# Block 1 of a two-block transformer: a step of the attention becomes a pair of heads on both sequences, in an order written out by hand

## The chip, the cores and the metric

The kernel runs on one core of a Trainium2 chip. The metric is the device time of one execution in microseconds (us). A profiled execution gives a trace: which instruction ran on which engine from when to when. Engines: PE (TensorE matmuls), PEld (its weight loads), DVE (VectorE), ACT (ScalarE), POOL (GpSimd), SP (SyncE, which issues the DMAs here). PSUM has eight banks of 128 partitions x 512 f32 numbers, into which PE writes.

## The reference

Sixteen sequences of 256 tokens with 128 channels go through two blocks. Block 0 (a feature-map attention and a six-layer local transformer as its feed-forward part) is not touched. Block 1, which the change rewrites, computes, for each sequence:

```
h = layernorm(x) * (1 + ca) + sa
q = (h @ Wq) in 16 heads of 64, * 64**-0.5;  k, v = h @ Wkv   # one k and v for all heads
sim = q @ k.T + relative_bias[head] * 8;  sim[j > i] = -max
x = x + ga * (softmax(sim) @ v, heads joined, @ Wout + bout)
h = layernorm(x) * (1 + cb) + sb
x = x + gb * (gelu(h @ w1 + b1) @ w2 + b2)                    # 128 -> 512 -> 128
```

The six vectors per sequence (`sa`, `ca`, ...) are worked out at the start of the kernel and stand in `mods`. Everything is f32.

## The kernel before

A **unit** is two sequences: x as a 128 x 512 tile, channels on partitions, the tokens of both sequences side by side. There are `NU` = 8 units. Block 0 runs first, in an order fixed by the program (`tc.manual_schedule`); its last stage leaves its result in tiles `z`, and x itself stands in DRAM (`xhome`).

**Between the blocks** (L1174 to L1187) x of all eight units is loaded (L1176, on SP), and the block's gated result is added in four DVE instructions per unit (L1182; `zpart` gives the two halves of the channels). After that block 1's weights are loaded on SP: `cWk` (two DMAs, L1205), `cWv`, `cWq` (L1200), the relative bias of the 8 head pairs in 32 DMAs (L1220, L1221), `cWo`, `dW1`, `dW2`: 38 DMAs. Their buffers come free when block 0's last matmuls are done.

**Block 1** (L1189 to L1435) works on 128 steps: unit, half of the head pairs `g`, sequence `s`, pair `j` in the half. Outside `manual_schedule` the program's order is only a wish: a list scheduler orders each engine's instructions. Its helpers:

- `prepare(u)`: layernorm and modulation (`normed` L227, `modulated` L256: mean by a matmul L230, subtraction on DVE L232, square on ACT L234, variance by matmuls L238, the power -0.5 on POOL L248, widened on POOL L215, transposed on PE L222, multiplied L253, scaled and shifted into `h` L261), then K (L1239, copied by ACT L1241) and V (L1244, L1252).
- `queries(p, h)`: one matmul for a pair of heads and both sequences (L1257), copied and scaled by ACT (L1259). Six buffers.
- `scores(p, s, ...)`: for one pair on one sequence four matmuls into two "sim" banks (L1271; of three), one bank per head; DVE adds the bias and takes the negated maximum in one instruction (L1285), ACT takes the exponential with its sum (L1296), DVE the reciprocal (L1305), POOL multiplies (L1307).
- `flip`: the probabilities are transposed, three 128 x 128 blocks per head into a bank of 384 columns (L1321), copied by DVE for one head (L1324) and by ACT for the other (L1326).
- `attend`: for four pairs together the product with V (L1334), copied by DVE (L1345) and ACT (L1347).
- The output projection is merged matmul by matmul over the next eight steps into a PSUM bank of its own, "y" (L1408).
- `closing(u)`: bias and gated add (L1353, L275 in `gated_add`), layernorm, the MLP (w1 L1362, copied by ACT L1364, gelu in place L1369, w2 L1373, bias L1375), gated add, transposes (L1380), copy (L1384), output DMA.

In a step the loop (L1396 on) first moves each running generator (`prepare` of the next unit, `closing` of the last) by one part, merges one matmul, computes scores, flips the step two back, and attends with the step three back when four pairs are complete. PSUM: four "mm" banks for all passing results, three "sim", one "y".

Of the kernel before, what the change touches and what calls it, by code (L numbers as in the profile page):

```python
# [10 lines left out]
F32 = mybir.dt.float32  # L11
# [33 lines left out]
def adaln_kernel(  # L45
# [9 lines left out]
    psy = ctx.enter_context(tc.tile_pool(name="psy", bufs=1, space=PSUM))  # L55
# [82 lines left out]
    xin = x_tiles(block.enter_context(tc.tile_pool(name="xa", bufs=1)))  # L138
# [87 lines left out]

    def normed(src):  # L227

        pm = bank()
        nc.tensor.matmul(pm, mean128, src, start=True, stop=True)  # L230
        xc = work("xc")
        nc.vector.tensor_tensor(two(xc), src, two(pm), ALU.subtract)  # L232
        sq = work("sqq")
        nc.scalar.activation(sq, xc, AF.Square)  # L234
        yield
        pv = bank()
        for t in range(4):
            nc.tensor.matmul(  # L238
                pv[:, t : t + 1],
                sq[:, t * 128 : (t + 1) * 128],  # L240
                mean128[:, 0:1],
                start=True,
                stop=True,
            )
        ve = small("ve", (128, 4))
        nc.vector.tensor_scalar(ve, pv[:, 0:4], 1e-5, None, ALU.add)
        rs = small("rs", (128, 4))
        nc.gpsimd.tensor_tensor(rs, ve, half[:, 0:4], ALU.pow)  # L248
        ex = widen(rs.unsqueeze(2), 1)
        yield  # L250
        rb = turned(ex)
        xn = work("xn")
        nc.vector.tensor_tensor(xn, xc, rb, ALU.mult)  # L253
        return xn

    def modulated(u, layer, j, dst):  # L256

        xn = yield from normed(two(xin[u]))
        for s in range(2):
            b = 2 * u + s  # L260
            nc.vector.tensor_scalar(  # L261
                dst[:, s * L : (s + 1) * L],
                xn[:, s * L : (s + 1) * L],
                mods[layer][:, j + 1, b : b + 1],
                mods[layer][:, j, b : b + 1],
                ALU.mult,
                ALU.add,
            )
# [904 lines left out]

    xin = x_tiles(ctx.enter_context(tc.tile_pool(name="xb", bufs=1)))  # L1174
    for u in range(NU):
        nc.sync.dma_start(xin[u], xhome[u])  # L1176
        for hf in range(2):
            r, zv = zpart(u, hf)
            for s in range(2):
                b = 2 * u + s  # L1180
                c = slice(s * L, (s + 1) * L)
                nc.vector.scalar_tensor_tensor(  # L1182
                    xin[u][r, c],
                    zv[:, s, :],
                    mods[0][r, 5, b : b + 1],
                    xin[u][r, c],
                    ALU.mult,  # L1187
                    ALU.add,
                )  # L1189


    with ExitStack() as es:
        pss = psum(es, 4, 3)
        wc = es.enter_context(tc.tile_pool(name="wc", bufs=1))
        stage["pool"] = es.enter_context(tc.tile_pool(name="kc", bufs=2))
        at = es.enter_context(tc.tile_pool(name="ct", bufs=2))

# [32 lines left out]

        inputs = {}

        def prepare(u):

            h = ctile("h", (128, 512))
            yield from modulated(u, 1, 0, h)
# [14 lines left out]
            v = ctile("v2", (128, 4, 64))  # L1251
            nc.scalar.copy(v.rearrange("p t d -> p (t d)"), pv[:, 0:256])  # L1252
            inputs[u] = h, kT, v

        def queries(p, h):
            pq = bank()
            nc.tensor.matmul(pq, wq[:, p * 128 : (p + 1) * 128], h, start=True, stop=True)  # L1257
            q = ctile("q2", (128, 512), 6)
            nc.scalar.activation(q, pq, AF.Copy, scale=0.125)  # L1259
            return q  # L1260
# [3 lines left out]
        def scores(p, s, q, kT):  # L1264
# [3 lines left out]
            for t in range(2):  # L1268
                for par in range(2):
                    r = slice(64 * par, 64 * par + 64)  # L1270
                    nc.tensor.matmul(  # L1271
                        sims[par][:, SPANS[t]],
                        q[r, c + 128 * t : c + 128 * t + 128],
                        kT[r, c : c + 128 * (t + 1)],
                        start=True,
                        stop=True,
                    )

# [3 lines left out]
            pr = ctile("pr2", (128, 2, 384), 3)  # L1282
            for par in range(2):
# [11 lines left out]
                for t in range(2):  # L1295
                    nc.scalar.activation(  # L1296
                        pr[:, par, SPANS[t]],
                        lg[:, par, SPANS[t]],
                        AF.Exp,
                        bias=nm[:, t, par : par + 1],  # L1300
                        scale=-1.0,
                        accum_out=ssum[:, t, par : par + 1],
                    )
            rsum = small("rsum2", (128, 2, 2))
# [8 lines left out]
            return pr  # L1313

        def flip(j, pr, prT):

            for par in range(2):
                pt = bank()
                for k in range(3):
                    c = slice(k * 128, (k + 1) * 128)  # L1320
                    nc.tensor.transpose(pt[:, c], pr[:, par, c], ident)  # L1321
                src = pt[:, 0:384].rearrange("p (k q) -> p k q", k=3)
                if par:
                    nc.vector.tensor_copy(prT[:, par, :, j, :], src)  # L1324
                else:
                    nc.scalar.copy(prT[:, par, :, j, :], src)  # L1326

        def attend(s, prT, v, oT):

            for t in range(2):  # L1330
                po = bank()
                for k in range(t + 1):
                    for par in range(2):
# [3 lines left out]
                            prT[:, par, t + k].rearrange("p j q -> p (j q)"),  # L1337
# [11 lines left out]
        def closing(u, oTs):  # L1349


            y = work("yo")
            nc.scalar.activation(y, oTs, AF.Identity, bias=vcol(_C_BOUT))  # L1353
# [3 lines left out]
            yield from modulated(u, 1, 3, h)  # L1357
            yield
            hid = []
            for c in range(4):  # L1360
# [3 lines left out]
                nc.scalar.copy(hc, ph)  # L1364
                hid.append(hc)
                if c % 2:
                    yield
            for c in range(4):
                nc.scalar.activation(hid[c], hid[c], AF.Gelu, bias=vcol(_D_B1 + c))  # L1369
            yield  # L1370
# [3 lines left out]
            y = work("yo")  # L1374
            nc.scalar.activation(y, py, AF.Identity, bias=vcol(_D_B2))  # L1375
            gated_add(u, 1, 5, y)
            yield
# [5 lines left out]
            xo = work("xt", (128, 4, 128))  # L1383
# [7 lines left out]
        steps = [  # L1391
            (u, g, s, j) for u in range(NU) for g in range(2) for s in range(2) for j in range(4)
        ]
        N = len(steps)
        per = N // NU
        for _ in prepare(0):  # L1396
            pass
        qs, prs, prTs, oTs, pys, running, merging = {}, {}, {}, {}, {}, [], []
        n = 0
        while n < N + 3 or running or merging:  # L1400
            for g_ in list(running):
                if next(g_, running) is running:
                    running.remove(g_)
            if merging:
                u, p = merging.pop(0)
                if p == 0:
                    pys[u] = psy.tile([128, 512], F32, tag="y", name="y")
                nc.tensor.matmul(  # L1408
                    pys[u], wout[:, p, :], oTs[u, p // 4][:, p % 4, :], start=(p == 0), stop=(p == 7)
                )  # L1410
                if p == 7:
                    running.append(closing(u, pys.pop(u)))
            if n < N:
                u, g, s, j = steps[n]
                p = 4 * g + j
                h, kT, _ = inputs[u]
                if s == 0:
                    qs[p] = queries(p, h)
                prs[n] = scores(p, s, qs[p], kT)
                if n % per == 4 and u + 1 < NU:  # L1420
                    running.append(prepare(u + 1))
            if 0 <= n - 2 < N:
                u, g, s, j = steps[n - 2]
                if j == 0:
                    prTs[u, g, s] = ctile("prT2", (128, 2, 3, 4, 128))
                    if s == 0:
                        oTs[u, g] = ctile("oT2", (128, 4, 512))
                flip(j, prs.pop(n - 2), prTs[u, g, s])
            if 0 <= n - 3 < N:
                u, g, s, j = steps[n - 3]  # L1430
                if j == 3:
                    attend(s, prTs.pop((u, g, s)), inputs[u][2], oTs[u, g])
                    if s == 1:
                        merging += [(u, 4 * g + a) for a in range(4)]
# [112 lines left out]
```

## Time and profile before

| what | us |
|---|---|
| device time, median of three runs | 4260.83 (4251.34, 4260.83, 4263.39) |
| profiled execution, in all | 4254.63 |
| its span (first to last instruction) | 4252.8 |
| block 1: first scores to the end | 3659.48 to 4252.8 |
| PE, ACT, DVE, POOL busy in the whole span | 3979.4, 2839.5, 2826.8, 2619.5 |

The span is what the trace shows; the rest of the profiled execution lies before and after it. The length of block 1's units is read from the starts of equal groups, such as the four w1 matmuls (L1362) of a unit: 3760.45, 3832.28, 3904.12, 3975.94, 4047.78, 4119.61. A line of the trace's timeline has the start, the time from the first start to the last end of a run of equal instructions, the engine, the line, the operation, result and operands with shapes, the number of instructions, and in brackets how long the engine had been idle and what released it. An f32 matmul is two instructions, so "x8" is four matmuls.

### The profile page before, as it was taken

What the parts mean: (1) busy time and instruction counts of PE and PEld (TensorE: products, weight loads), DVE (VectorE), ACT (ScalarE), POOL (GpSimd) and SP (SyncE); (2) the same over time, 40 slices, a digit from 0 to 9 for tenths busy, and PEclk for the clock granted to TensorE, in tenths of its full rate; (3) what the DMA queues carried; (4) which work ended last, traced back from release to release, by engine and by line L of the source; (5) the groups of instructions that cost most, each with busy time, mean ns of one, the idle gap of its engine ahead of it and who ended that gap; (6) DMA issues with size and microseconds to landing.
All of it is one profiled execution on the core that took longest, in us unless ns stands there. A gap on an engine that the chain in (4) does not pass through costs nothing.

```text
span 4252.8 us, 118394 instructions
## 1 busy us (share of the span) xinstructions
PE 3979.4 (94%) x45491; PEld 2576.8 (61%) x45491; DVE 2826.8 (66%) x6003; ACT 2839.5 (67%) x9800; POOL 2619.5 (62%) x3326
## 2 busy tenths in 40 slices
PE   7867999999999999999999999999999998899998
PEld 4534666666666666666666666666666666454544
DVE  6746667777676777667676767776676765455554
ACT  4535666766767666666766666766667665578785
POOL 5446666676666776676766677666767673343432
PEclk9889999999999999999999999999999999999999
DMA  1334344444444444444444444444444441100000
GB/s 40 40 95 106 100 108 102 113 103 106 109 100 113 106 108 104 106 115 104 104 107 104 114 101 109 106 105 113 105 104 100 108 102 58 46 3 6 4 6 6
DMA packets 193548, 371.06 MB, mean 87 GB/s; under 512 B 42538, under 2 KB 83417, under 8 KB 192985
## 3 DMA queue, kind: packets, MB, share of 16 engines
q1 hardware_dynamic: 192984, 363.50, 34.2%
q8 instruction: 360, 5.90, 0.6%
q14 instruction: 204, 1.66, 0.1%
HBM read 127.92 MB, written 8.91 MB: 32 GB/s over the span
## 4 chain that ended last, share of the span: by engine, by line
PE 45%; DVE 23%; ACT 19%; issue 6%; POOL 5%; DMA 1%; SPq 0%; POOLq 0%; DVEq 0%; ACTq 0%
ACT pr L907 10%; PE mm L948 9%; PE sim L885 7%; DVE sent L745 6%; PE mm L764 4%; ACT sq L743 4%; PE mm L930 4%; POOL pr L922 4%; DVE k L748 3%; DVE q L748 3%; PE mm L740 3%; DVE mx L897 2%; PE mm L847 2%; PE mm L1334 2%; DVE nb L899 2%
## 5 line engine op out<-in xcount | busy, mean ns | idle before, releaser
L907 ACT ACTIVATE pr<-sim,nb,rq 128x64 f32<-128x64 f32 x3072 | 1229.5, 451 | 336.9 <-DVE nb L899 328.9
L922 POOL TENSOR_TENSOR pr<-pr,rsum 128x512 f32<-128x512 f32 x384 | 398.3, 1042 | 809.9 <-DVE rsum L920 769.4
L907 ACT ACTIVATION_READ_ACCUMULATOR pr<-sim,nb,rq 128x1 f32 x3072 | 773.9, 252 | 0.0
L969 PEld LDWEIGHTS y<-zx,wvo 128*128 128x128 f32 x6144 | 715.7, 192 | 91.5 <-issue 88.7
L969 PE MATMUL y<-zx,wvo 128*128 128x128 f32 x6144 | 717.5, 275 | 1.3 <-ACT zx L963 1.2
L740 PE MATMUL mm<-z,wqk 128*128 128x512 f32 x1536 | 706.4, 602 | 8.6 <-DMA wqk<-in_L_ffn_Wqkv_dram 6.7
L745 DVE SCALAR_TENSOR_TENSOR sent<-mm,vec,rope 128x512 f32<-128x512 f32 x768 | 570.6, 743 | 118.4 <-ACT sq L743 110.2
L756 POOL TENSOR_TENSOR k<-k,got 128x512 f32<-128x512 f32 x384 | 496.1, 1292 | 0.0
L756 POOL TENSOR_TENSOR q<-q,got 128x512 f32<-128x512 f32 x384 | 487.9, 1271 | 12.7 <-DMA got<-sent 10.6
L837 POOL TENSOR_TENSOR k<-k,kn 128x512 f32<-128x512 f32 x384 | 481.8, 1274 | 19.6 <-DMA kn<-rkh 19.6
L743 ACT ACTIVATE sq<-mm 128x512 f32<-128x512 f32 x768 | 475.0, 618 | 24.0 <-PE mm L740 23.9
L740 PEld LDWEIGHTS mm<-z,wqk 128*128 128x128 f32 x1536 | 278.1, 191 | 323.1 <-issue 237.4
L961 DVE COPY zx<-mm 128x512 f32<-128x512 f32 x384 | 265.6, 692 | 256.7 <-PE mm L948 256.7
L963 ACT COPY zx<-mm 128x512 f32<-128x512 f32 x384 | 225.2, 586 | 287.8 <-PE mm L948 287.8
L1307 POOL TENSOR_TENSOR pr<-pr,rsum 128x256 f32<-128x256 f32 (+1 forms) x256 | 206.1, 826 | 317.3 <-DVE rsum L1305 309.9
L948 PE MATMUL mm<-prT,xw 64*128 64x256 f32 x3072 | 389.5, 390 | 3.4 <-DVE zx L961 2.0
L897 DVE TENSOR_REDUCE mx<-sim 128x8 f32<-128x512 f32 x384 | 263.2, 685 | 176.1 <-PE sim L885 176.1
L948 PEld LDWEIGHTS mm<-prT,xw 64*128 64x128 f32 x3072 | 293.5, 187 | 119.8 <-issue 90.4
L930 PE MATMUL mm<-ident,pr 128*128 128x128 f32 x1536 | 246.2, 284 | 106.5 <-POOL pr L922 76.6
L930 PEld LDWEIGHTS mm<-ident,pr 128*128 128x128 f32 x1536 | 175.4, 143 | 272.3 <-POOL pr L922 243.4
L885 PEld LDWEIGHTS sim<-k,q 64*32 64x32 f32 x24576 | 264.9, 105 | 86.7 <-issue 58.4
L885 PE MATMUL sim<-k,q 64*32 64x64 f32 x24576 | 298.8, 226 | 19.1 <-issue 9.8
(250 smaller groups left out, 6545.2 us busy)
## 6 DMA issues: line engine op xcount, KB each, us to landing
got<-sent SPq DMA_DIRECT2D x1536, 128.0 KB
kn<-rkh SPq DMA_DIRECT2D x768, 128.0 KB
xw<-xw SPq DMA_DIRECT2D x96, 256.0 KB
wqk<-in_L_ffn_Wqkv_dram SPq DMA_DIRECT2D x48, 128.0 KB
bhome<-brow SPq DMA_DIRECT2D x1, 3072.0 KB
wv<-in_L_ffn_Wqkv_dram SPq DMA_DIRECT2D x12, 256.0 KB
wo<-in_L_ffn_Wo_dram SPq DMA_DIRECT2D x12, 256.0 KB
xt<-in_x_dram SPq DMA_DIRECT2D x8, 256.0 KB
```

Source lines behind the costliest of these rows:

```text
L740: nc.tensor.matmul(pp, wqk[:, j, :], xs, start=True, stop=True)
L743: nc.scalar.activation(sq, pp, AF.Square)
L745: nc.vector.scalar_tensor_tensor(two(sent[:, j, :]), two(pp), scale, tab[1], ALU.mult, ALU.mult)
L756: nc.gpsimd.tensor_tensor(r, r, two(got[:, j, :]), ALU.add)
L837: nc.gpsimd.tensor_tensor(k, k, two(kn), ALU.mult)
L885: nc.tensor.matmul(sims[par][32 * c : 32 * c + 32, c0 : c0 + 64], q[r, s, t0 : t0 + 32], k[r, s, t0 : t0 + 64], start=False, stop=True, sk ...
L897: nc.vector.tensor_reduce(mx, sim.rearrange("p (b k) -> p b k", b=8), AX.X, ALU.max)
L907: nc.scalar.activation(pr[:, x, st, par, :], sims[par][:, b * 64 : (b + 1) * 64], AF.Exp, bias=nbs[par][:, b : b + 1], scale=rn[:, par, b ...
L922: nc.gpsimd.tensor_tensor(prf, prf, rsum.unsqueeze(2).to_broadcast([128, 8, 64]), ALU.mult)
L930: nc.tensor.transpose(pt[:, st * 128 : (st + 1) * 128], pr[:, x, st].rearrange("p h k -> p (h k)"), ident,)
L948: nc.tensor.matmul(pz[par][:, w * 256 : (w + 1) * 256], xw[r, (2 * k + w) % 8, :], prT[r, :, 64 * k + 32 * w : 64 * k + 32 * w + 32], star ...
L969: nc.tensor.matmul(py[:, j * 128 : (j + 1) * 128], vo[:, h, :], zx[:, h % 2, h // 2, :], start=(h == 0), stop=(h == 2 * NP - 1), skip_grou ...
```

## The change

Block 1 goes under `manual_schedule` for PE, DVE, ACT and POOL, so each engine runs in program order (SP's DMAs are still placed by the scheduler). The loop is written anew around it:

- A step is one head pair on **both** sequences: 64 steps, 8 per unit. PSUM is four "mm" and four "sim" banks; the "y" bank is closed after block 0. Per step: 8 score matmuls in a row into the four "sim" banks, the query of the next step, twelve transposes of the step before into three full banks of four. DVE copies two of these banks, ACT the middle one.
- The query is scaled and copied by DVE instead of ACT; two buffers.
- `softmax` and `divided` are separate: the reciprocal and the division of the first sequence stand behind the bias reductions of both, those of the second behind the query and the transposes.
- `attend` runs in the steps 6, 7, 9 and 10 after the unit's first. The output projection is the first two parts of `closing`, four matmuls each, in an "mm" bank. gelu reads PSUM and does the copy, four in a row. Five yields stand between w1 and w2 (one in the last unit), and one more ahead of the output.
- The generators run last in a step, after attend.
- x of a unit is loaded in `prepare(u)` (six buffers, in place of eight tiles loaded together), and the four residual updates stand there (`leave`) as a part of their own. `prepare(0)` stands after the weights in the program.

```diff
-    xin = x_tiles(ctx.enter_context(tc.tile_pool(name="xb", bufs=1)))
-    for u in range(NU):
-        nc.sync.dma_start(xin[u], xhome[u])
-        for hf in range(2):
...
+    accum.close()
...
+        es.enter_context(tc.manual_schedule(engines=ENGINES))
+        pss = psum(es, 4, 4)
...
         def prepare(u):
+            xin[u] = ctile("x", (128, 512), 6)
+            nc.sync.dma_start(xin[u], xhome[u])
+            yield
+            leave(u)
+            yield
             h = ctile("h", (128, 512))
...
-            q = ctile("q2", (128, 512), 6)
-            nc.scalar.activation(q, pq, AF.Copy, scale=0.125)
+            q = ctile("q2", (128, 512), 2)
+            nc.vector.tensor_scalar(q, pq, 0.125, None, ALU.mult)
...
-            pr = ctile("pr2", (128, 2, 384), 3)
+            pr = ctile("pr2", (128, 2, 384), 5)
...
+            for g in range(3):
                 pt = bank()
+                for a in range(4):
+                    nc.tensor.transpose(pt[:, a * 128 : (a + 1) * 128], blocks[4 * g + a], ident)
+                dst = prT[:, 4 * g : 4 * g + 4, j, :]
+                src = pt.rearrange("p (k q) -> p k q", k=4)
+                if g == 1:
+                    nc.scalar.copy(dst, src)
                 else:
+                    nc.vector.tensor_copy(dst, src)
...
+            py = bank()
+            for p in range(NP):
+                nc.tensor.matmul(
+                    py, wout[:, p, :], oTs[p // 4][:, p % 4, :], start=(p == 0), stop=(p == NP - 1)
+                )
+                if p == 3:
+                    yield
...
-                nc.scalar.copy(hc, ph)
+                nc.scalar.activation(hc, ph, AF.Gelu, bias=vcol(_D_B1 + c))
                 hid.append(hc)
-                if c % 2:
+            if u + 1 < NU:
+                for _ in range(5):
                     yield
...
+        while n <= N + 4 or running:
+            u, p = divmod(n, NP)
             if n < N:
                 h, kT, _ = inputs[u]
+                sims = [scores(s, q, kT) for s in range(2)]
+                prs[n] = []
+                for s in range(2):
+                    pr, ssum = softmax(p, sims[s])
+                    prs[n].append((pr, ssum))
+                    if s:
+                        divided(*prs[n][0])
+                if n + 1 < N:
+                    u2, p2 = divmod(n + 1, NP)
+                    q = queries(p2, inputs[u2][0])
+            if 0 <= n - 1 < N:
...
+                flip(j, [v[0] for v in prs.pop(n - 1)], prTs[u1, g])
+            if n < N:
+                divided(*prs[n][1])
+            for lag, g, s in ((6, 0, 0), (7, 0, 1), (9, 1, 0), (10, 1, 1)):
+                v, r = divmod(n - lag, NP)
+                if r == 0 and 0 <= v < NU:
+                    attend(s, prTs[v, g], inputs[v][2], oTs[v, g])
...
+            for parts in list(running):
+                if next(parts, running) is running:
+                    running.remove(parts)
+            v, r = divmod(n - 10, NP)
+            if r == 0 and 0 <= v < NU:
+                running.append(closing(v, [oTs.pop((v, g)) for g in range(2)]))
+            if p == 0 and u + 1 < NU:
+                running.append(prepare(u + 1))
             n += 1
```

More of the change, by code (lines that the diff above doesn't have):

```diff
@@ L54, in adaln_kernel @@
     sm = ctx.enter_context(tc.tile_pool(name="sm", bufs=4))
-    psy = ctx.enter_context(tc.tile_pool(name="psy", bufs=1, space=PSUM))
+    accum = ctx.enter_context(ExitStack())
+    psy = accum.enter_context(tc.tile_pool(name="psy", bufs=1, space=PSUM))
     def bank():
@@ L137, in adaln_kernel @@
     psum(block, 7, 0)
-    xin = x_tiles(block.enter_context(tc.tile_pool(name="xa", bufs=1)))
+    xin = dict(enumerate(x_tiles(block.enter_context(tc.tile_pool(name="xa", bufs=1)))))
     stage["pool"] = block.enter_context(tc.tile_pool(name="ka", bufs=3))
@@ L225, in turned @@
         return rb
[L227 to L268, printed above, removed]
     def gated_add(u, layer, j, y):
@@ L1172, in adaln_kernel @@
         stage["flat"] = None
-    xin = x_tiles(ctx.enter_context(tc.tile_pool(name="xb", bufs=1)))
-    for u in range(NU):
-        nc.sync.dma_start(xin[u], xhome[u])
-        for hf in range(2):
[L1178 to L1189, printed above, removed]
+    accum.close()
     with ExitStack() as es:
-        pss = psum(es, 4, 3)
+        es.enter_context(tc.manual_schedule(engines=ENGINES))
+        pss = psum(es, 4, 4)
         wc = es.enter_context(tc.tile_pool(name="wc", bufs=1))
@@ L1196, in adaln_kernel @@
         at = es.enter_context(tc.tile_pool(name="ct", bufs=2))
+        xin.clear()
         def load1(name, shape, src):
@@ L1229, in ctile, with leave @@
             return at.tile(list(shape), F32, tag=tag, name=tag, bufs=bufs)
+        def leave(u):
+            for hf in range(2):
+                r, zv = zpart(u, hf)
+                for s in range(2):
+                    b = 2 * u + s
+                    c = slice(s * L, (s + 1) * L)
+                    nc.vector.scalar_tensor_tensor(
+                        xin[u][r, c],
+                        zv[:, s, :],
+                        mods[0][r, 5, b : b + 1],
+                        xin[u][r, c],
+                        ALU.mult,
+                        ALU.add,
+                    )
@@ new lines, in modulated @@
+        def modulated(u, j, h):
+            pm = bank()
+            nc.tensor.matmul(pm, mean128, xin[u], start=True, stop=True)
+            xc = ctile("xc", (128, 512), 3)
+            nc.vector.tensor_tensor(xc, xin[u], pm, ALU.subtract)
+            sq = ctile("sqq", (128, 512), 1)
+            nc.scalar.activation(sq, xc, AF.Square)
+            yield
+            pv = bank()
+            for t in range(4):
+                nc.tensor.matmul(
+                    pv[:, t : t + 1],
+                    sq[:, t * 128 : (t + 1) * 128],
+                    mean128[:, 0:1],
+                    start=True,
+                    stop=True,
+                )
+            ve = small("ve", (128, 4))
+            nc.vector.tensor_scalar(ve, pv[:, 0:4], 1e-5, None, ALU.add)
+            rs = small("rs", (128, 4))
+            nc.gpsimd.tensor_tensor(rs, ve, half[:, 0:4], ALU.pow)
+            ex = ctile("ex", (128, 4, 128), 1)
+            nc.gpsimd.tensor_copy(ex, rs.unsqueeze(2).to_broadcast([128, 4, 128]))
+            yield
+            rb = bank()
+            for t in range(4):
+                nc.tensor.transpose(rb[:, t * 128 : (t + 1) * 128], ex[:, t], ident)
+            nc.vector.tensor_tensor(xc, xc, rb, ALU.mult)
+            for s in range(2):
+                b = 2 * u + s
+                c = slice(s * L, (s + 1) * L)
+                nc.vector.tensor_scalar(
+                    h[:, c],
+                    xc[:, c],
+                    mods[1][:, j + 1, b : b + 1],
+                    mods[1][:, j, b : b + 1],
+                    ALU.mult,
+                    ALU.add,
+                )
@@ L1231, in adaln_kernel @@
         inputs = {}
         def prepare(u):
+            xin[u] = ctile("x", (128, 512), 6)
+            nc.sync.dma_start(xin[u], xhome[u])
+            yield
+            leave(u)
+            yield
             h = ctile("h", (128, 512))
-            yield from modulated(u, 1, 0, h)
+            yield from modulated(u, 0, h)
+            inputs[u] = [h]
             yield
@@ L1252, in prepare @@
             nc.scalar.copy(v.rearrange("p t d -> p (t d)"), pv[:, 0:256])
-            inputs[u] = h, kT, v
+            inputs[u] += [kT, v]
         def queries(p, h):
@@ L1257, in queries, with scores @@
             nc.tensor.matmul(pq, wq[:, p * 128 : (p + 1) * 128], h, start=True, stop=True)
-            q = ctile("q2", (128, 512), 6)
-            nc.scalar.activation(q, pq, AF.Copy, scale=0.125)
+            q = ctile("q2", (128, 512), 2)
+            nc.vector.tensor_scalar(q, pq, 0.125, None, ALU.mult)
             return q
         SPANS = (slice(0, 128), slice(128, 384))
-        def scores(p, s, q, kT):
+        def scores(s, q, kT):
             c = s * L
@@ L1277, in scores, with softmax @@
                     )
+            return sims
+        def softmax(p, sims):
             lg = ctile("lg2", (128, 2, 384))
@@ L1303, in scores, with divided @@
                     )
+            return pr, ssum
+        def divided(pr, ssum):
             rsum = small("rsum2", (128, 2, 2))
@@ L1312, in scores, with flip @@
                 )
-            return pr
-        def flip(j, pr, prT):
-            for par in range(2):
-                pt = bank()
[L1319 to L1324, printed above, removed]
+        def flip(j, prs, prT):
+            blocks = [
+                pr[:, par, k * 128 : (k + 1) * 128]
+                for pr in prs
+                for par in range(2)
+                for k in range(3)
+            ]
+            for g in range(3):
+                pt = bank()
+                for a in range(4):
[4 more added lines that the diff above has]
+                    nc.scalar.copy(dst, src)
                 else:
-                    nc.scalar.copy(prT[:, par, :, j, :], src)
+                    nc.vector.tensor_copy(dst, src)
         def attend(s, prT, v, oT):
@@ L1336, in attend @@
                             v[:, 2 * s + k, :],
-                            prT[:, par, t + k].rearrange("p j q -> p (j q)"),
+                            prT[:, 6 * s + 3 * par + t + k].rearrange("p j q -> p (j q)"),
                             start=(k == 0),
@@ L1349, in closing @@
         def closing(u, oTs):
-            y = work("yo")
-            nc.scalar.activation(y, oTs, AF.Identity, bias=vcol(_C_BOUT))
+            py = bank()
+            for p in range(NP):
+                nc.tensor.matmul(
+                    py, wout[:, p, :], oTs[p // 4][:, p % 4, :], start=(p == 0), stop=(p == NP - 1)
+                )
+                if p == 3:
+                    yield
+            y = ctile("yo", (128, 512), 1)
+            nc.scalar.activation(y, py, AF.Identity, bias=vcol(_C_BOUT))
             gated_add(u, 1, 2, y)
@@ L1356, in closing @@
             h = ctile("h3", (128, 512), 1)
-            yield from modulated(u, 1, 3, h)
+            yield from modulated(u, 3, h)
             yield
@@ L1363, in closing @@
                 hc = ctile("hid", (128, 512), 4)
-                nc.scalar.copy(hc, ph)
+                nc.scalar.activation(hc, ph, AF.Gelu, bias=vcol(_D_B1 + c))
                 hid.append(hc)
-                if c % 2:
+            if u + 1 < NU:
+                for _ in range(5):
                     yield
-            for c in range(4):
-                nc.scalar.activation(hid[c], hid[c], AF.Gelu, bias=vcol(_D_B1 + c))
-            yield
+            else:
+                yield
             py = bank()
@@ L1373, in closing @@
                 nc.tensor.matmul(py, w2[:, c, :], hid[c], start=(c == 0), stop=(c == 3))
-            y = work("yo")
+            y = ctile("yo", (128, 512), 1)
             nc.scalar.activation(y, py, AF.Identity, bias=vcol(_D_B2))
             gated_add(u, 1, 5, y)
+            yield
             yield
@@ L1382, in closing @@
                 )
-            xo = work("xt", (128, 4, 128))
+            xo = ctile("xo", (128, 4, 128), 1)
             nc.scalar.copy(xo.rearrange("p t d -> p (t d)"), pt)
@@ L1387, in closing @@
             )
[L1391 to L1395, printed above, removed]
+        N = NU * NP
         for _ in prepare(0):
             pass
-        qs, prs, prTs, oTs, pys, running, merging = {}, {}, {}, {}, {}, [], []
+        q = queries(0, inputs[0][0])
+        prs, prTs, oTs, running = {}, {}, {}, []
         n = 0
[L1400 to L1412, printed above, removed]
+        while n <= N + 4 or running:
+            u, p = divmod(n, NP)
@@ L1413, in adaln_kernel @@
             if n < N:
-                u, g, s, j = steps[n]
-                p = 4 * g + j
                 h, kT, _ = inputs[u]
[L1417 to L1423, printed above, removed]
-                if j == 0:
[L1425 to L1434, printed above, removed]
+                sims = [scores(s, q, kT) for s in range(2)]
+                prs[n] = []
+                for s in range(2):
+                    pr, ssum = softmax(p, sims[s])
+                    prs[n].append((pr, ssum))
+                    if s:
+                        divided(*prs[n][0])
@@ new lines, in adaln_kernel @@
+                if n + 1 < N:
+                    u2, p2 = divmod(n + 1, NP)
+                    q = queries(p2, inputs[u2][0])
+            if 0 <= n - 1 < N:
+                u1, p1 = divmod(n - 1, NP)
+                g, j = divmod(p1, 4)
+                if j == 0:
+                    prTs[u1, g] = ctile("prT2", (128, 12, 4, 128))
+                    oTs[u1, g] = ctile("oT2", (128, 4, 512), 3)
+                flip(j, [v[0] for v in prs.pop(n - 1)], prTs[u1, g])
+            if n < N:
+                divided(*prs[n][1])
@@ new lines, in adaln_kernel @@
+            for lag, g, s in ((6, 0, 0), (7, 0, 1), (9, 1, 0), (10, 1, 1)):
+                v, r = divmod(n - lag, NP)
+                if r == 0 and 0 <= v < NU:
+                    attend(s, prTs[v, g], inputs[v][2], oTs[v, g])
+                    if s:
+                        prTs.pop((v, g))
+            for parts in list(running):
[4 more added lines that the diff above has]
+                running.append(closing(v, [oTs.pop((v, g)) for g in range(2)]))
```

## The prediction

> **What bounds the kernel now.** First the engines' busy times in two whole units of block 1 (columns: window, length, then busy us of PE, weight loads, DVE, ACT, POOL, then clock):
>
> ```profile
> 3832.28:3904.12 71.84, 69.51 (x363) 35.97 (x363) 39.61 (x178) 55.29 (x175) 28.96 (x37) 1.00 0.02 5
> 3904.12:3975.94 71.82, 69.50 (x363) 35.97 (x363) 39.53 (x178) 55.30 (x175) 28.94 (x37) 1.00 0.02 5
> ```
>
> PE is busy for 69.5 of 71.83 us, the same in each unit; ACT and DVE have slack. Block 1 takes 593.3 us, from its first scores at 3659.48 to the end at 4252.8; all before it stays as it was. Next, PE's own order in the timeline (start, duration):
>
> ```profile
> 3839.39 1.02 PE L1408 MATMUL y<-oT,cWo 128*128 128x512 f32 x2
> 3840.34 0.93 PE L1271 MATMUL sim<-k,q 64*128 64x128 f32 x8
> 3841.20 0.87 PE L1321 MATMUL mm<-ident,pr 128*128 128x128 f32 x6
> 3841.91 1.02 PE L1408 MATMUL y<-oT,cWo 128*128 128x512 f32 x2
> 3842.86 0.93 PE L1271 MATMUL sim<-k,q 64*128 64x128 f32 x8
> 3844.47 0.77 PE L1321 MATMUL mm<-ident,pr 128*128 128x128 f32 x5 [0.42 <-POOL pr L1307]
> ```
>
> Work of other stages stands between scores and transposes, so PE almost never waits (the table of PE's waits names 2.2 us in a whole unit, the largest for POOL's probabilities, 1.0): with such gaps as the 0.42 and the leads at a change of operation I count 11 us per unit in which it does no row of work; 61 are work. (f32 runs in two rows, "x8" is four matmuls.) Prices from starts: a 512-column matmul 0.86 (3839.39 to 3840.34 less a lead of 0.095), four score matmuls 0.86 (3840.34 to 3841.20), a transpose 0.11. Last, the entry:
>
> ```profile
> 3572.76 3.68 SPq L1176 DMA_DIRECT2D x<-xh  x8
> ...
> 3642.70 0.81 SPq L1205 DMA_DIRECT2D cWk<-in_L_attn_Wkv_dram  x2
> ...
> 3644.28 1.10 PE L230 MATMUL mm<-x,mean 128*128 128x512 f32 x2 [1.72 <-DVE z L984]
> ...
> 3659.48 2.57 PE L1271 MATMUL sim<-k,q 64*128 64x128 f32 x16
> ...
> 3660.17 1.05 SPq L1200 DMA_DIRECT2D dW<-in_L_ffn_w_dram  x2
> ```
>
> x is fetched 70 us ahead; the 38 weight and bias transfers, 0.47 apart, run beside the first layernorm.
>
> **Entry: +23.** In the new program the first unit's x is queued on SP behind those 38, issued near 3661.3. The last of the 38 landed at 3665.5 at some 210 GB/s; x's 256 KB take 1.2 more: 3666.7. L1182's work, which stood in DVE's queue at 3577.7 ahead of block 0's reciprocal at 3581.55, is gone there: PE waited 3.2 for that, I take 1.7 of it: 3665. Then four residual updates (L1182's four at 3644.17 took 1.77) and 0.25 to the next engine: 3667.1. From L230 to the first scores before took 15.2 (3644.28 to 3659.48); one query less now, but an idle PE's slow rows (below) for longer, 0.4 more on balance: 3682.7, **+23.2**. PE has nothing to hide it. The later units' x is issued two steps, some 14 us, ahead of its use, beside idle queues, and costs nothing; without that cover a load's 2 us plus its 1.2 of transfer would stand in front of p2's updates. The bounds: if x landed before the others, +4 (the updates, less the 1.7, plus PE's wake); if x waited its own 2 us and the idle PE ran its rows at half speed through the entry (they took 0.85 instead of 0.43 at 3644 to 3657 already), +27.
>
> **PE's work per unit: 61.6.** Scores: eight in a row are not in the trace of a full unit. Bounds: two groups as now, 1.91, and the merged row of 3659.48, sixteen in 2.57, so 1.29. I take 1.5, between them and nearer the row: 0.3 saved on each of eight steps, 2.5 with leads. Queries, transposes, attend, merge and MLP keep their matmul count. PE has 61.6 per unit if nothing makes it wait; of the 11 us of gaps it loses the queries' second home and about half the leads.
>
> **What makes it wait.** The order is fixed now: a step is 8 scores, the next query, 12 transposes, then attend or the parts of prepare and closing. The prices of the other engines:
>
> ```profile
> L1324 DVE COPY prT<-mm 128x384 f32<-128x384 f32 x128 | 70.8, 553 | 46.8 <-PE mm L1321 46.7
> L1259 ACT ACTIVATE q<-mm 128x512 f32<-128x512 f32 x64 | 37.8, 591 | 13.7 <-PE mm L1257 13.7
> L1345 DVE COPY oT<-mm 128x512 f32<-128x512 f32 x32 | 21.9, 685 | 32.5 <-PE mm L1334 32.5
> L275 DVE SCALAR_TENSOR_TENSOR x<-yo,mod,x 128x256 f32<-128x256 f32 x32 | 20.2, 670 | 18.9 <-ACT yo L1375 14.3 <-ACT yo L1353 4.6
> L1307 POOL TENSOR_TENSOR pr<-pr,rsum 128x512 f32<-128x512 f32 x128 | 133.0, 1039 | 0.0
> ```
>
> A pair-step's DVE work: eight bias reductions (0.56 per bank), two reciprocals, the query's copy (0.69, moved from ACT), two copies of 512 columns (0.69 by the oT row; before two of 0.55), an oT copy in half of the steps. DVE grows from 39.6 by 5.5 (queries), 2.2 (wider copies), 1.9 (the residual updates per unit) to 49; ACT falls from 55.3 by 4.7, 2.6 (8 × (2 × 0.46 − 0.59)), 2.4 (hidden copies gone, gelu reads PSUM) and 2.6 (one pair of table loads) to 43. Neither is a bound by its sum. By its place it is: the four "mm" banks are taken in turn, so the first part of a step takes the bank that the step's query left, and waits for DVE's copy of it. That copy stands behind eight reductions and the first reciprocal, which waits for four exps:
>
> ```profile
> 3841.30 0.29 DVE L1285 CUSTOM_DVE_ANT_0 lg<-sim,bias 128x128 f32<-128x128 f32 x1 [1.57 <-PE sim L1271]
> ...
> 3842.46 0.18 DVE L1305 RECIPROCAL rsum<-ssum 128x4 f32<-128x4 f32 x1 [0.31 <-ACT pr L1296]
> ```
>
> From the first score the reductions start at 0.96 (3840.34 to 3841.30) and end at 3.2; the reciprocal ends by 3.36, the copy at 4.05; the part may start at 4.12, where PE is ready at 3.72 (scores 1.5, query 0.86, transposes 1.32). The steps of a unit, p0 to p7 for its eight pairs, with the parts' own matmuls added: p0 (w1) 4.12 + 3.44 = 7.6; p1, p2 (attend) 6.8 each; p3 (mean, four merges) 8.5; p4 (variance, four merges; its third transpose bank waits for the query too) 9.2; p5 (w2, transposes, mean) 8.9; p6 (attend, K, V) 9.6; p7 (attend, output) 7.9: **65.4**.
>
> Then what DVE or ACT hand on late to the next step's scores: p0 0.5 (the layernorm's end of p7), p1 1.4 (four gelus and two table loads ahead of its exps), p3 1.6 (oT copy and four updates, 0.68 + 1.9, less slack), p5 0.8 (gated add), p6 1.8 (gated add, multiply, two halves of h, subtraction): 6.1 (single updates taken at 0.48, between L1182's 0.44 and the gated row's 0.67, which holds waits). (POOL's two normalisations per step, 3.2 us, and the layernorm's 1.0 + 0.6 fit into a step of 6.8 or more; if they did not, the transposes of the next step would wait.) Gaps of 1, as before: **72.5** against 71.83. The saving in scores and in changes of operation is spent on these waits. If all cover for the lateness is there (PE's slack after the copy is used again by the next step) 65.4 + 1 remains; if the lateness counts half more, 75.5.
>
> [...] The row first: ACT's table load at 3847.01 takes 1.28 and the exp behind it starts at 3848.30, so a change of table costs 1.28 there. [...]
>
> **The sum** on the profiled execution (span 4252.8, 4254.63 with what lies around it). First scores 3682.7; steps 0 to 10, 4.5 to 6.9 each as they carry few parts, 66.5; steps 11 to 15 are 5/8 of a unit, 43.5; five units × 72.5 = 362.5; steps 56 to 62, 58.5; the last step and tail 53 (before: last scores 4209.08 to the end 43.7; now all eight merges and unit 6's MLP stand there): 4266.7, that is **+13.9**. The profiled execution lies 6.2 below the median 4260.83, inside the runs' 4251.34 to 4263.39; on the median **4275**. Its own range: entry −5 to +4, scores ±0.4 × 6.5 units, waits −1.5 to +1 per unit, tail ±3: 4258 to 4288.
>
> **Rivals.** About 6.5 units' worth of time hangs on the length of a unit.
> - **PE stays the bound (faster).** The copies run ahead, the query's copy is done when needed, and the lateness is used up by PE's own longer parts. For it: DVE has 22 us of slack per unit, ACT 28, and the list-ordered program kept PE at 97%. Against: in a fixed order nothing fills a wait. Full: unit 61.6 + 1 = 62.7, 9.8 × 6.5 = 64 less: 4211. Half: 67.6: 4243. It decides once a unit falls below 70.4 (13.9 / 6.5 = 2.1 below 72.5); a gain of 0.3% needs 68.4. Chance 0.26.
> - **Lateness adds up (slower still).** DVE's in-order queue, POOL's 1.61 per half-step (0.57 + 1.04) and the exps chain from step to step, 75.5 per unit: 4295; with the late end of the entry's bounds 4300. For it: each engine's order is fixed alike. Against: short steps p1 and p2 let DVE catch up. Chance 0.2.
> - **x comes early (no change).** SP's issues or transfers overlap so that x lands with the first weights: entry +4, 4256. For it: 16 engines share the queue. Against: one queue, in order. Chance 0.07.
> - **It doesn't do what it says**: excluded; the compiled order has eight score matmuls in a row in every step.
>
> **How the numbers follow.** Forecast 0.47, rivals 0.26, 0.2, 0.07. Below 4232 lies the upper part of the first rival (0.12), above 4302 the worst of the second (0.08): range 4232 to 4302. A measurement tells 0.3%, 12.8 us, from no change: faster (below 4248) 0.24: nearly all of the first rival; slower (above 4273.6): the second rival and 0.28 of the forecast's 0.47, 0.48; same 0.28.
>
> **What would show it.** First scores near 3682 (entry); w1 groups 72.5 apart; waits of PE's parts on the query's copy, 0.4 each; PE waiting in p1 for exps behind gelu and in p6 for reductions behind gated adds; scores 1.5 per eight. I am wrong if units repeat every 68 or less, or if x lands before 3650.

## The result, and the profile after

The changed kernel takes 4270.07 us, median of ten runs (4262.48 to 4273.53), against 4260.20 for the kernel before (4251.34 to 4263.39): a ratio of 1.0025, 95% interval 1.0015 to 1.0035. So it is slower by about 10 us, a little less than the 0.3% that was taken as the bound of no change. The profiled execution has a span of 4269.0 us, against 4252.8. All kernels' spans also differ by a few us in block 0, which none of them touches; below, block 1 is counted from its first scores, and the entry from block 0's last matmul.

Two whole units of block 1 in the changed kernel (columns as in the prediction: PE, weight loads, DVE, ACT, POOL, clock):

```profile
3949.10:4020.89 71.79, 64.00 (x363) 36.38 (x363) 45.09 (x191) 43.65 (x154) 29.00 (x37) 1.00 0.02 5
4020.89:4092.68 71.79, 63.99 (x362) 36.38 (x363) 45.08 (x191) 43.65 (x154) 28.99 (x37) 1.00 0.02 5
```

A unit takes 71.8 as before, but now PE is busy for only 64.0 of it: the change took 5.5 us of PE time out, and put waits in. PE's timeline over parts of the steps p7 and p1 (p0 to p7 are a unit's eight pairs) shows where (L1278 scores, L1264 query, L1340 transposes, L1354 attend):

```profile
3864.43 1.58 PE L1278 MATMUL sim<-k,q 64*128 64x128 f32 x16
3865.94 1.12 PE L1264 MATMUL mm<-h,cWq 128*128 128x512 f32 x2
3866.91 1.47 PE L1340 MATMUL mm<-ident,pr 128*128 128x128 f32 x12
3868.58 2.79 PE L1354 MATMUL mm<-prT,v 128*64 128x512 f32 x12 [0.20 <-DVE q L1266]
...
3886.12 2.79 PE L1354 MATMUL mm<-prT,v 128*64 128x512 f32 x12 [1.55 <-DVE q L1266]
```

Eight score matmuls take 1.51 (3864.43 to 3865.94), as estimated. From the first score to the part it is 4.15 (3868.58), and PE waits for "q", the query's copy, which frees the part's bank; behind the gelus it waits 1.55. The table of PE's waits in block 1 (us in all, times, longest) has little else:

```profile
PE mm L1354 <- DVE q L1266: 26.6, 29, 2.1
PE mm L1194 <- DVE q L1266: 13.7, 7, 3.1
PE mm L1399 <- DVE q L1266: 5.2, 6, 0.9
PE mm L1340 <- DVE q L1266: 4.5, 7, 0.6
PE mm L1388 <- DVE q L1266: 4.3, 6, 0.7
```

In DVE's own timeline the copy stands where the working had put it, behind the first reciprocal, with the transposed banks' copies behind it:

```profile
3867.77 0.18 DVE L1319 RECIPROCAL rsum<-ssum 128x4 f32<-128x4 f32 x1
3867.86 0.66 DVE L1266 TENSOR_SCALAR q<-mm 128x512 f32<-128x512 f32 x1
3868.44 1.28 DVE L1346 COPY prT<-mm 128x512 f32<-128x512 f32 x2
```

And the entry, from the timelines of SP and PE:

```profile
3641.71 0.83 SPq L1149 DMA_DIRECT2D cWk<-in_L_attn_Wkv_dram  x2
...
3660.37 211.94 SPq L1237 DMA_DIRECT2D x<-xh  x7
```

```profile
3638.89 2.74 PE L1012 MATMUL mm<-fg,w 128*128 128x512 f32 x6
3667.94 2.05 PE L1194 MATMUL mm<-x,mean 128*128 128x512 f32 x2 [26.31 <-DMA x<-xh]
...
3684.54 2.94 PE L1278 MATMUL sim<-k,q 64*128 64x128 f32 x16 [0.88 <-DVE q L1266]
```

The first x is issued at 3660.37, behind the weights and biases (they are 39 transfers, not the 38 counted ahead of the prediction), and PE stands still for 26.3 us. First scores come at 3684.54, 25.1 later than before; from there to the end it is 584.5, 8.8 less than before.

### The profile page after: what moved, and what is told of

Its sections match the earlier page's. It is cut to its first block, busy times and chain, and to the rows that moved or that the text cites. A ratio compares the mean times of both kernels' runs of the same rounds, so it can differ in the third digit from the quotient of the medians.

```text
span 4269.0 us, 118217 instructions
## 1 busy us (share of the span) xinstructions
PE 3936.5 (92%) x45491; PEld 2579.3 (60%) x45491; DVE 2863.3 (67%) x6067; ACT 2746.6 (64%) x9624; POOL 2622.5 (61%) x3326
## 4 chain that ended last, share of the span: by engine, by line
PE 42%; DVE 25%; ACT 19%; issue 8%; POOL 5%; DMA 1%; SPq 0%; POOLq 0%; DVEq 0%; ACTq 0%
ACT pr L865 11%; PE mm L906 9%; PE sim L843 7%; DVE sent L703 6%; PE mm L722 4%; ACT sq L701 4%; POOL pr L880 4%; PE mm L888 4%; DVE k L706 3%; DVE q L706 3%; PE mm L698 3%; DVE mx L855 3%; PE mm L805 2%; DVE lg L1296 2%; PE mm L1354 2%
```

## The experiments

Each is named by its label. Steps p0 to p7 are a unit's eight pairs; "the unit" is the distance of equal steps. Ratios are to the kernel before, run on the same chip, with 95% intervals; the changed kernel has 1.0025 (1.0015 to 1.0035).

My theory was that of the forecast: the entry costs some 25 us, and in a unit the part of each step waits for a bank that DVE's (or ACT's) in-order queue frees late, so that PE's shorter work doesn't count. The rivals: the entry is set by something else; PE, or DVE's work as a whole, is the bound.

**e1_x_first**: x of the first unit is loaded ahead of the weights.

```diff
+        xin[0] = at.tile([128, 512], F32, tag="x", name="x", bufs=6)
+        nc.sync.dma_start(xin[0], xhome[0])
         wk2 = wc.tile([128, 2, 64], F32, tag="cWk", name="cWk")
```

> The changed kernel with only the load of the first unit's x moved ahead of the 38 weight and bias transfers. My theory (the entry costs 25 us because that load is queued last): x is issued near 3641.7, lands near 3645, the four updates end near 3647, first scores near 3663.5 instead of 3684.5, units unchanged at 71.8: 21 us less than the changed kernel, near 4249. Rival (the transfers share 16 DMA engines and the first unit is set by the weights or by the cold PE): first scores later than 3675, less than 10 us gained.

Measured: ratio 0.9978 (0.9968 to 0.9987). From block 0's last group of matmuls to the first scores it is 24.3 us (3642.65 to 3666.90) against 45.7 (3638.89 to 3684.54) in the changed kernel and 19.7 (3639.82 to 3659.48) before: 21.4 gained. PE's first matmul on x, and the first scores, in this run:

```profile
3650.31 2.04 PE L1196 MATMUL mm<-x,mean 128*128 128x512 f32 x2 [4.92 <-DVE x L1184]
...
3666.90 2.93 PE L1281 MATMUL sim<-k,q 64*128 64x128 f32 x16 [0.88 <-DVE q L1269]
```

The units stay at 71.8. The entry was the queue on SP, and it is the whole loss: without it the change is faster than the kernel before.

**e2_q_between**: DVE copies the query between the two sequences' reductions; PE's order is unchanged.

```diff
                     if s:
                         divided(*prs[n][0])
-                if n + 1 < N:
-                    u2, p2 = divmod(n + 1, NP)
-                    q = queries(p2, inputs[u2][0])
+                    elif n + 1 < N:
+                        u2, p2 = divmod(n + 1, NP)
+                        q = queries(p2, inputs[u2][0])
```

> The changed kernel with DVE's copy of the next query put between the bias reductions of the two sequences; PE's order is the same. My theory (the parts wait for the bank that DVE's in-order queue frees late): the waits on that copy, 58 us in block 1, go almost entirely; by the working of the prediction 0.4 per step and some of the lateness, 3.2 to 6.7 per unit: units of 65 to 68.6, 21 to 43 us less, 4227 to 4249. Rival (PE with its leads and gaps is the bound, or ACT): units stay at 71.8 within 0.5, time within 4 us of the changed kernel.

Measured: ratio 1.0019 (1.0009 to 1.0028), units of 71.3. The waits on the query went from 58 to 8 us, as expected; most of the gain did not come. PE's waits and its timeline in p4 of this kernel:

```profile
PE mm L1354 <- DVE prT L1346: 13.8, 28, 0.9
PE mm L1202 <- DVE prT L1346: 7.2, 6, 1.2
```

```profile
3903.55 1.61 PE L1340 MATMUL mm<-ident,pr 128*128 128x128 f32 x12
3906.36 1.02 PE L1202 MATMUL mm<-mean,sqq 128*128 128x1 f32 x8 [1.20 <-DVE prT L1346]
3907.24 5.38 PE L1373 MATMUL mm<-oT,cWo 128*128 128x512 f32 x8
```

Two things: the next bank in turn is freed by the next copy in the same queue (prT), so the wait moved there (28 us of waits on prT, where the changed kernel had none); and in p4 four merges (L1373) took 5.38 us in place of 3.68, because rows ran at half speed (granted clock 0.51 from 3908 to 3911). p0, p1, p3, p5 and p6 gained 0.3 to 1.1 each, p2 and p7 lost 0.19 each, p4 lost 2.15. In unit 6 no row ran slowly: there p4 took 9.79 and the unit 69.60, a gain of 2.2. The time and the unit lie within the rival's bounds, but its reason is not the one: waits on ACT are 2 us in all, and e3, next, speaks against PE. My figure of 3.2 to 6.7 per unit fell: I had moved one copy and forgotten the one behind it, and had not thought of the clock.

**e3_extra_transposes**: the third bank's four transposes are done twice.

```diff
-                    nc.tensor.transpose(pt[:, a * 128 : (a + 1) * 128], blocks[4 * g + a], ident)
+                    for _ in range(2 if g == 2 else 1):
+                        nc.tensor.transpose(pt[:, a * 128 : (a + 1) * 128], blocks[4 * g + a], ident)
```

> The changed kernel with the four transposes of the third bank done twice, 0.44 us more PE work in each of 64 steps, in front of the part that waits. My theory: hidden in the waits of p0, p1, p3, p5 and p6 (0.7 to 1.8 each); +0.24 in p2 and p7, +0.44 in p4: 0.9 per unit, about +6 us. Rival (PE is the bound): +3.5 per unit, +23 to +28 us.

Measured: units of 72.3, so +0.5 for 3.5 us of added PE work, 0.17 in each of p2, p4 and p7 (I had expected 0.9, with 0.44 in p4); p0, p1, p3, p5 and p6 do not move by 0.02. PE is not the bound. (Ratio 1.0048, 1.0033 to 1.0063; its interval is too wide to tell +3 from +6 us.)

**e4_no_gelu**: the gelu is left out, and with it two table loads per unit.

```diff
-                nc.scalar.activation(hc, ph, AF.Gelu, bias=vcol(_D_B1 + c))
+                nc.scalar.activation(hc, ph, AF.Identity, bias=vcol(_D_B1 + c))
```

> The changed kernel with the gelu left out (the four instructions add the bias only, so they need no table load). My theory: p1's step falls from 8.23 to the 6.87 of p2, 1.36 per unit, and the tail loses a load or two: 10 to 13 us less. Rival (ACT's slack hides the loads, or they cost more than the 1.28 of their rows): units within 0.3 of 71.8, or more than 2.7 less per unit.

Measured: p1 6.87 in place of 8.23, as expected, the unit 70.43. The ratio is 1.0012 (1.0003 to 1.0022), some 5 us less, about half of the expectation: six units gave 1.36 each, but in the profiled execution one unit's p6 took 13.25 in place of 11.23, and the tail, from which I expected the rest, took 53.2 in place of 52.0.

**e10_no_leave**: the four residual updates of units 1 to 7 are left out.

```diff
-            leave(u)
+            if u == 0:
+                leave(u)
```

> The changed kernel with the residual updates of units 1 to 7 (four DVE instructions of a unit, in p2) left out. It measures the lateness that p2 hands to p3. My theory: p3 falls from 10.20 by 1.6 to 1.8, to 8.4 to 8.6, the other steps stay within 0.1: units of 70.1, 10 to 13 us less. Rival (p3 waits for something else, the mean or the merges' bank): p3 stays above 9.5.

Measured: p3 8.63 in place of 10.20, the other steps within 0.02 in most units; units of 70.23 in three of five, the others 70.5; ratio 0.9994 (0.9984 to 1.0003), 13 us less. The lateness that p2 hands to p3 is 1.57. In the first unit p3 fell by more, from 9.15 to 5.36.

**e7_query_on_act**: one part undone, the query is copied by ACT again (with the order of e2).

```diff
-            nc.vector.tensor_scalar(q, pq, 0.125, None, ALU.mult)
+            nc.scalar.activation(q, pq, AF.Copy, scale=0.125)
```

> One part undone: the query's copy is on ACT again, between the exps of the two sequences; DVE loses 0.69 per step, PE's order is as in the changed kernel. My theory: the copy ends near 4.0 as it did on DVE, so p1, p2, p7 stay within 0.3, while the steps in which DVE came late (p3, p5, p6, p0) each gain up to 0.6: units of 69 to 70.5, 8 to 18 us less. Rival (it is only the place of the query's copy, not DVE's load): units within 0.7 of 71.8.

Measured: 69.57 in units 2 and 4; three other units took 71.2. Ratio 1.0014 (1.0005 to 1.0023). Against the changed kernel p0, p3, p5 and p6 gained 0.38 each, p4 0.65, p2 and p7 0.27; p1 lost 0.48. The 69.57 lies where I expected the unit, though the time fell by some 5 us and not by 8 to 18. It does not show that DVE's load counts: this run has e2's order too, and e2's one unit at full clock took 69.60 with the copy on DVE. The place of the copy, the rival's reason, gives as much alone. In the longer units p1 took 10.1 to 10.4 in place of 8.70; PE had waited just as long in both, and then ran slowly:

```profile
4090.17 1.47 PE L1340 MATMUL mm<-ident,pr 128*128 128x128 f32 x12
4093.67 4.49 PE L1354 MATMUL mm<-prT,v 128*64 128x512 f32 x12 [2.03 <-ACT q L1266]
```

Twelve rows of attend took 4.49, where an undisturbed attend takes 2.79.

**e5_copies_early**: the order of a step is rewritten so that each bank is copied before PE needs it. `turns` gives one transposed bank at a time: the first and third are copied by DVE, the second by ACT.

```diff
+                sims = [scores(s, q, kT) for s in range(2)]
+                prs[n] = [softmax(p, sims[0])]
+                next(turns, None)
+                next(turns, None)
+                prs[n].append(softmax(p, sims[1]))
+                divided(*prs[n][0])
+            for _ in turns:
+                pass
+            if n < N:
+                if n + 1 < N:
+                    u2, p2 = divmod(n + 1, NP)
+                    q = queries(p2, inputs[u2][0])
+                divided(*prs[n][1])
```

> The changed kernel with the order of a step rewritten: scores, the twelve transposes, then the query, then parts; DVE: reductions of the first sequence, copy of transposed bank 1, reductions of the second, reciprocal, copy of bank 3, query copy; ACT: exps of the first sequence, copy of bank 2, exps of the second. So every bank that a part takes was copied before PE comes to it. My theory (the place in DVE's and ACT's queue of what frees the next bank sets the unit): PE's waits for DVE copies all but go, parts start 3.8 after the first score instead of 4.12, lateness of 6.1 per unit falls to about 2: units of 63 to 67, first scores as in the changed kernel, 30 to 55 us less. Rival (DVE's work as a whole, or PE's clock, which fell to half in three rows of each unit of the run with the query copy in between, takes it back): units of 70 or more, less than 12 us gained.

Measured: ratio 0.9924 (0.9907 to 0.9941), 43 us less than the changed kernel, units of 65.28. The same instructions, in another order; a whole unit and the largest of the waits that are left:

```profile
3949.10:4014.38 65.28, 63.14 (x363) 35.52 (x362) 45.31 (x191) 43.70 (x155) 28.95 (x36) 1.00 0.02 5
```

```profile
PE mm L1355 <- ACT prT L1344: 7.6, 7, 1.3
PE sim L1278 <- DVE q L1266: 6.8, 7, 1.4
PE mm L1194 <- DVE prT L1346: 3.9, 7, 0.9
```

DVE and ACT have the same busy time per unit as in the changed kernel (45.1 and 43.7) and PE is at 97%. Their load as a whole was not the bound; their order was.

**e6_early_x_too**: e5, with ACT copying the third bank instead of the second in p1, and x in a pool of its own that is free while block 0 still runs.

```diff
+    xb = ctx.enter_context(tc.tile_pool(name="xb", bufs=1))
+    for u in range(2):
+        xin[u] = xb.tile([128, 512], F32, tag="x", name="x", bufs=6)
+        nc.sync.dma_start(xin[u], xhome[u])
...
-                if g == 1:
+                if g == onact:
                     nc.scalar.copy(dst, src)
...
+                turns = flip(j, [v[0] for v in prs.pop(n - 1)], prTs[u1, g], 2 if p == 1 else 1)
```

> The order of e5 (with ACT copying the third bank in place of the second behind the gelus, in p1) and x of the first units in a pool of its own, loaded while block 0 ends, as the kernel before did. My theory: first scores 17 to 18 us after block 0's last matmul ends (42.9 in the changed kernel, 21.5 with x first), 25 us less by that, and 30 to 55 by the order: 55 to 80 us below the changed kernel, ratio to before 0.983 to 0.990. Rival as for e5: 0.994 or more.

Measured: 4194.68 us, ratio 0.9856 (0.9842 to 0.9871): it beats both kernels. From the start of block 0's last group to the first scores it is 19.2 (16.4 from its end, where I had expected 17 to 18); the unit is 64.45, with p1 6.56 in place of 8.02 and p2 7.19 in place of 6.56.

**e8_scores_apart**: e6 with the pairing of the scores undone.

```diff
-                sims = [scores(s, q, kT) for s in range(2)]
+                sims = [scores(0, q, kT)]
                 prs[n] = [softmax(p, sims[0])]
                 next(turns, None)
+                sims.append(scores(1, q, kT))
                 next(turns, None)
```

> The kernel of e6 with the pairing of the scores undone: the first transposed bank stands between the score matmuls of the two sequences, all else equal. It measures the term 'eight score matmuls in a row save 0.3 per step' where PE sets the step. My theory: 0.3 to 0.4 per step come back, units of 66.5 to 67.5 in place of 64.45, 15 to 20 us more than e6. Rival (joining saves nothing, or DVE's chain from the first score still sets the step): units within 0.6 of 64.45.

Measured: units of 65.72, +1.27; ratio 0.9884 (0.9870 to 0.9899). p0, p1, p5 and p7 lost 0.35 each, as forecast per step; p4 0.18; p3 and p6 nothing, and p2 even gained 0.28, since other waits end there. Both expectations missed: pairing is worth what I had priced, in about half of the steps, and that with PE already at 97%.

**e9_before_late_x**: the kernel before, with its x tiles in a pool opened after the weights and the eight loads and 32 updates behind the weights.

```diff
+        xin = x_tiles(es.enter_context(tc.tile_pool(name="xb", bufs=1)))
+        for u in range(NU):
+            nc.sync.dma_start(xin[u], xhome[u])
...
```

> The kernel before with one thing of the change alone: its x tiles lie in a pool opened after the weights, and their eight loads and 32 updates stand behind the weights in the program, so that SP issues them last. My theory: the first unit's x lands near 3666, first scores near 3682 to 3685 in place of 3659.5, units unchanged: 23 to 26 us more than before, ratio 1.0054 to 1.0062. Rival (a list scheduler fills the hole, or the later loads cost as well): less than 15 or more than 32 us.

Measured: ratio 1.0080 (1.0065 to 1.0095), some 34 us. PE's timeline:

```profile
3673.01 2.04 PE L230 MATMUL mm<-x,mean 128*128 128x512 f32 x2 [26.56 <-DVE x L1220]
3686.94 1.87 PE L238 MATMUL mm<-mean,sqq 128*128 128x1 f32 x8 [11.88 <-ACT sqq L234]
```

The first 26.56 is the entry of the changed kernel over again (26.31). The 11.88 is new: the updates of the other seven units stand ahead of the first subtraction in DVE's order. So the rival about the later loads holds here, by their updates; the units stay at 71.83. The changed kernel avoids it since its updates, not its loads, stand unit by unit: SP issues six of its loads together, from 3660.37 to 3663.61.

## Why the prediction was right

The forecast was 13.9 us more, the measured difference 10 (median) and 16.2 (profiled spans); the mechanism was the one forecast, and the runs confirm its two halves. Step by step:

- **Entry, +23.2**: measured 25.1, and e1 took 21.4 of it back by one DMA's place. Right. Wrong was that the later units' x is issued two steps ahead: six of the loads stand together at the entry. No later update waits for one, so it cost nothing that the trace shows. The 2 us and the 1.2 that I gave a load without cover were my estimate: in the kernel before, the first load of x was issued at 3572.76 and DVE began on it at 3575.39, 2.63 us in all.
- **Scores in a row, 1.5**: measured 1.51, with some luck: the lower bound of 1.29 read sixteen matmuls into the row at 3659.48, whose x16 is eight, in 2.57. The saving of 2.5 per unit exists only where PE sets the step: e8 found 1.27 at 97% PE, and e3 shows that in the changed kernel PE's time counted in three steps of eight.
- **PE's work, 61.6**: PE was busy for 64.0 per unit, and for 63.1 in e5. The sum did not rest on it, but the full case of the first rival, 62.7, did.
- **The part waits for the query's copy, 4.12**: measured 4.15. Right for the changed kernel. That moving this copy alone would free the unit, as I expected of e2, was wrong: the copies stand in one queue, and only moving all of them (e5) moved the unit.
- **Steps with lateness** (forecast against measured): p0 8.1, 8.30; p1 8.2, 8.23; p2 6.8, 6.87; p3 10.1, 10.20; p4 9.2, 9.33; p5 9.7, 9.74; p6 11.4, 11.23; p7 7.9, 7.90. Sum 71.5 (these rounded terms give 71.4) against 71.8; the 1.0 that I added for small gaps was not there (0.3), so the unit came out at 71.8 and not 72.5. e4 measured p1's term as 1.36 (forecast 1.4), e10 p3's as 1.57 (1.6).
- **DVE's sum, 49**: measured 45.1; why it is less was not followed. Nothing hung on it.
- **The sum from the first scores, 584.0**: measured 584.5, which flatters the working: steps 0 to 10 took 71.3, not 66.5 (two of them took 9.15 and 12.22, where 4.5 to 6.9 was the forecast: PE waited long for the copy there, 3.08 and 1.95, and rows ran at half speed behind that: the granted clock was 0.50 from 3704.5 to 3711.2 and 0.51 from 3724.9 to 3728.4); steps 11 to 15 44.7 (43.5, though 5/8 of 72.5 is 45.3); five units 359.3 (362.5); steps 56 to 62 57.2 (58.5); the tail 52.0 (53). The misses cancel, which is luck.

Why a rewriting that frees 5.5 us of PE per unit moves the time so little is thus settled: its gain was turned into waits for copies in DVE's and ACT's queues, and the gain outside the whole units (8.8 from the first scores on) was paid at the entry with 25. The forecast's rival of a faster unit was open to the same instructions in another order: e5's 65.3 lies between its half and its full case.

A change of table: ACT's rows in the changed kernel show a table load of 1.28 (3878.32), as in the kernel before, right behind a copy that ends at 3878.30, and the gelu behind it starts at 3879.61. Leaving two loads out gained 1.36 per unit in all (e4).

## What to carry to other kernels

When an order is written out by hand, find for every bank (or buffer) that PE takes next the instruction that frees it, and what stands ahead of that instruction in its engine's queue: DVE and ACT, busy for 45.1 and 43.7 of a unit's 71.8 us, set the time here because the freeing copies stood behind waits. Move all copies of such a chain at once, since moving one only handed the wait to the next (e2: 58 to 8 us on q, none to 28 on prT). And count DMA issues as part of the order: 39 issues of 0.47 us ahead of the one that the first matmul needs cost 21 us, and moving that one load ahead of them won it back.

## What the runs showed of the hardware

I had not expected PE's clock to matter inside a busy stage. In e7 PE waited the same 2.03 us ahead of an attend in seven steps (once in p6, six times in p1). In two of them nothing followed; in five, two to four of the next rows of 512 columns (an f32 matmul runs as two rows) took 0.84 in place of 0.42, some 1.4 to 1.7 us lost. In e2 a wait of 1.20 and eight matmuls of one column were followed by slow rows in p4 of five units of six. In the changed kernel slow rows followed one wait of 1.95 in p6 (the attend took 4.49), and none followed six of 1.82 to 2.14 (2.79).

The granted clock in the trace differs in the same way. Here are two stretches of e7 (columns as above): the first lies behind the wait from 4091.64 to 4093.67, the second behind the equal one from 3950.81 to 3952.84.

```profile
4094.60:4097.50 2.90, 2.90 (x10) 0.73 (x6) 0.18 (x1) 1.72 (x6) 2.18 (x3) 0.50 0.00 0
3954.58:3957.99 3.41, 3.41 (x24) 1.71 (x21) 2.34 (x13) 1.96 (x7) 1.61 (x2) 1.00 0.02 5
```

Behind the first wait the clock was 0.50 and the attend took 4.49; behind the second it was 1.00, and the attend took 2.79:

```profile
3952.84 2.79 PE L1354 MATMUL mm<-prT,v 128*64 128x512 f32 x12 [2.03 <-ACT q L1266]
```

So in these runs the length of a wait alone did not tell what came behind it. What decides it was not shown: no run varied the waits on purpose.
